# Softmax sums folded over partitions by accumulating DMAs, and kept in two running sums

## The chip, the cores and the metric

One core of one Trainium2 chip. The metric is the device time of one launch in microseconds (us). The run times and the profile of the kernel before are given below. Engines are named as in the profile: PE is TensorE (PEld its weight loads), DVE is VectorE, ACT is ScalarE, POOL is GpSimd, SP is SyncE, which only issues DMAs here.

## The reference, cut to what matters

Two graph layers over 16 images of 1024 nodes and 256 channels. The change concerns the attention of the first layer (4 heads of 64 channels), its softmax above all:

```python
h = jnp.maximum(_layernorm(x, axis=-1), 0.0)
# layer 0: q from a graph product with adj, k and v from h @ kv_w
q = jnp.transpose(g, (0, 2, 1)).reshape(B, N, h, hd).transpose(0, 2, 1, 3)
scale = (1.0 + 1e-06) / (np.sqrt(hd) + 1e-06)
attn = jax.nn.softmax(jnp.einsum('bhnd,bhmd->bhnm', q, k) * scale, axis=-1)
out = jnp.einsum('bhnm,bhmd->bhnd', attn, v)
# then x = x + out; layer 1: another layernorm, A_hat @ h, two linear layers with batch norms
```

The kernel takes the exps without subtracting a maximum, multiplies them with v, and divides by their sum at the end. Smallest and largest inverse sum are kept (`most`, `least`), and a general version runs afterwards if they leave a safe range.

## The kernel before, in words

The kernel is one long loop over the images b. The order of instructions on every engine is written out by hand: what the program says first on an engine runs first there, and an instruction that waits holds all that stand behind it on that engine. Data lies transposed: in the scores, the partitions are the keys m (8 blocks of 128), and the free axis holds 2 heads x 512 queries.

Attention of one image has four steps, each for half of the queries (g = 0, 1) and a pair of heads. Step s does this:

- `scores(s)` (L743 to L760): for each of the eight key blocks, TensorE computes the scores into PSUM (`f_s`), ScalarE takes the exp into `f_p` (128x1024, eight buffers), and VectorE adds the blocks up into `f_acc` (128x1024, two buffers): one add of two blocks (L757), and six that each add to the same running sum (L760).
- `partial(s)` (L768, L776): `f_acc` holds, per partition, the sum over 8 keys; the sum over the 128 partitions remains. VectorE transposes blocks of 32x32 (128x1024 to `f_sums`) and reduces over 32. That leaves four partial sums for each query, one per group of 32 partitions (`f_red`).
- `values(s)` (L784, L797): TensorE multiplies the exps with v into `f_o`, and VectorE transposes the product into `f_oT`.

`finish(g)` inverts the sums of one half and scales: `collect` (four ScalarE copies bring the four groups' sums side by side on 32 partitions, L811), `invert` (VectorE: reduce L817, reciprocal L818, `most` and `least`), `spread` (four ScalarE copies bring the inverses to the partitions that need them, L826), `scale` (VectorE multiplies `f_oT`, L835, and SyncE moves blocks of 32 partitions to their places with 16 DMAs, L852) and `add` (VectorE, L860). For g = 0 they run in the middle of step 2 and at its end; those of g = 1, with the `add` of g = 0, are handed on as `left` to what follows attention.

What follows is the graph product of the next image, `graph` for b = 0 and `graph_seven` for b = 1 to 14. `graph_seven` is a Strassen-like scheme of seven products: ScalarE and VectorE make eight weight blocks (`differences(b, c)`, then `masked(b, c)`, L361), VectorE forms the sums t1 to t4 of them (L557 to L569), and TensorE runs `plain(0)`, `plain(1)` (L514) and then the products `m1` to `m_7` (L576), in an order given in the source. In VectorE's order stand `masked(b, 2)`, `masked(b, 3)`, then `collect` and `invert` of the attention just done, then `masked(b, 4)`, the t sums, `masked(b, 5)` and on to `scale` and `masked(b, 7)`. At its start, SyncE is given loads: `sums_h` (buffer tag "sums"), `sums_c` (in a buffer of tag "acc"), two blocks of hT, para, `sums`, and with `load_more` six blocks of 512 KB (L915). After it come the keys and values, the linear layers of the image before (`linear1`, `linear1_seven`), and the next attention. For the last image (b = 15) no graph product is left, and `collect` and `invert` stand before `sums_of_h` of `linear1`.

GpSimd does little: the inverse roots of the norms (L260), and stores and copies of DMAs (`turn_h`, L379; `pair_sums`, L482; `turn_h_aside`, L496).

Of the kernel before, what the change touches and what calls it, by code (L numbers as in the profile page):

```python
# [10 lines left out]
F32 = mybir.dt.float32  # L11
AF = mybir.ActivationFunctionType
ALU = mybir.AluOpType
AX = mybir.AxisListType
# [15 lines left out]
def fast_path(  # L30
# [62 lines left out]

    RECS = HEADS * 512 // 32
    most = const.tile([32, RECS], F32, tag="most", name="f_most")
    nc.vector.memset(most, 1.0)
    least = const.tile([32, RECS], F32, tag="least", name="f_least")
    nc.vector.memset(least, 1.0)
# [77 lines left out]
    with ExitStack() as stage:  # L176
# [324 lines left out]
        def graph_seven(b, left, norm, load_more, last):  # L501
# [26 lines left out]
            nc.sync.dma_start(sums_h, gs_d[b][:, 0:8].rearrange("p (s n) q -> p s n q", s=4))  # L528
            nc.sync.dma_start(sums_c, gs_d[b][:, 8:12])
            hT = []  # L530
# [4 lines left out]
            qT = big.tile([P, CC, N], F32, tag="qT", name=f"f_qT_{b}")  # L535
            nc.sync.dma_start(qT, para_v)
            nc.sync.dma_start(sums, kvs_d)
            load_more()
            kT = big.tile([P, CC, N], F32, tag="kT", name=f"f_kT_{b}")
# [192 lines left out]
        def attention(b, qT, kT, v, hooks):  # L732

            steps = [(g, pair) for g in range(NH) for pair in range(HEADS // 2)]
            p_of, acc_of, oT_of, o_of, red_of = {}, {}, {}, {}, {}

            def scores(s, within=None):
                g, pair = steps[s]
                for m in range(NC):
# [13 lines left out]
                    if m == 1:  # L753
                        acc = pp.tile(
                            [P, 2, 512], F32, tag="acc", name=f"f_acc_{b}_{s}", bufs=2
                        )
                        nc.vector.tensor_add(acc, p_of[s, 0], p)  # L757
                        acc_of[s] = acc
                    elif m > 1:
                        nc.vector.tensor_add(acc_of[s], acc_of[s], p)  # L760
                    if m == 5 and within:
                        within()

            def partial(s):

                g, pair = steps[s]
                t = ow.tile([P, 2, 16, 32], F32, tag="sums", name=f"f_sums_{b}_{s}")
                nc.vector.transpose(  # L768
                    t.rearrange("p e j i -> p (e j i)"),
                    acc_of.pop(s).rearrange("p e q -> p (e q)"),  # L770
                )
                if pair == 0:
                    red_of[g] = small.tile(
                        [P, HEADS // 2, 2, 16], F32, tag="red", name=f"f_red_{b}_{g}", bufs=1
                    )
                nc.vector.tensor_reduce(red_of[g][:, pair], t, AX.X, ALU.add)  # L776

# [24 lines left out]
            def finish(g):  # L802
# [4 lines left out]
                def collect():  # L807
                    t = ow.tile([32, RECS, 4], F32, tag="parts", name=f"f_parts_{b}_{g}")
                    red = red_of.pop(g).rearrange("p h e j -> p (h e j)")
                    for a in range(4):  # L810
                        nc.scalar.copy(t[:, :, a], red[ts(a, 32), :])  # L811
                    kept["parts"] = t

                def invert():
                    t = small.tile([32, HEADS // 2, 2, 16], F32, tag="rec", name=f"f_rec_{b}_{g}")
                    every = t.rearrange("p h e j -> p (h e j)")
                    nc.vector.tensor_reduce(every, kept["parts"], AX.X, ALU.add)  # L817
                    nc.vector.reciprocal(every, every)  # L818
                    nc.vector.tensor_tensor(most, most, every, ALU.max)
                    nc.vector.tensor_tensor(least, least, every, ALU.min)  # L820
                    kept["rec"] = t

                def spread():
                    t = small.tile([P, HEADS // 2, 4, 4], F32, tag="recs", name=f"f_recs_{b}_{g}")
                    for a in range(4):
                        nc.scalar.copy(  # L826
                            t[ts(a, 32)].rearrange("p h j c -> p h c j"),
                            kept["rec"][:, :, a // 2].rearrange("p h (c j) -> p h c j", c=4),
                        )
                    kept["recs"] = t  # L830
# [37 lines left out]
            for i in range(len(steps)):  # L868
                scores(i, collect if i == 2 else None)
                for step in hooks.get(i, ()):  # L870
                    step()
                if i == 2:
                    invert()
                    spread()
                partial(i)
                if i == 2:
                    scale()
                values(i)
# [419 lines left out]
        with tc.manual_schedule(engines={ENG.PE, ENG.Activation, ENG.DVE, ENG.Pool, ENG.SP}):  # L1298
# [73 lines left out]
            for b in range(B):  # L1372
# [15 lines left out]
                def more(c):  # L1388
# [4 lines left out]
                    0: [  # L1393
                        lambda: turn_h(b + 1), more(2), left[0], left[1], left[2], more(3),
                        left[3], left[4], more(4),
                    ],
# [94 lines left out]
    with ExitStack() as stage:  # L1491
# [21 lines left out]
        with tc.manual_schedule(engines={ENG.PE, ENG.Activation, ENG.DVE, ENG.Pool, ENG.SP}):  # L1513
# [118 lines left out]
            def flag_bad():  # L1632

                bad = const.tile([32, 4], F32, tag="bad", name="f_bad")
                nc.vector.tensor_reduce(bad[:, 0:1], most, AX.X, ALU.max)
# [735 lines left out]
```

## Time and profile before

| | |
|---|---|
| median of 3 runs | 2397.92 us (2396.44 to 2398.54) |
| span of the profiled execution | 2396.9 us |
| what lies around that span, if it is taken as a median run | 1.0 us |
| one image in the middle (856.21 to 987.40 us) | 131.2 us: TensorE busy 131.0, VectorE 112.2, ScalarE 73.2, GpSimd 9.4 |
| of it attention, four steps | 56.3 us |
| mean clock granted to TensorE | 0.995 |
| transposes and reduces of the sums (L768, L776) | 64 each, 79.2 and 78.1 us of VectorE |

The page gives busy time per engine, 40 slices of the span, the chain of work that ended last, the costliest groups of instructions (line, engine, operation, output from inputs, shapes, count, then busy time and mean ns of one, then the engine's idle time before them and what ended it) and the DMA issues (output from input, issuing queue, count, KB each, median us from issue to landing). A timeline has start and length in us, then engine, line, operation, tiles and count; in square brackets stands the idle time before, and what ended it. "SPq" and "POOLq" are DMAs issued by SyncE and GpSimd.

### The profile page before, as it was taken

What the parts mean: (1) busy time and instruction counts of PE and PEld (TensorE: products, weight loads), DVE (VectorE), ACT (ScalarE), POOL (GpSimd) and SP (SyncE); (2) the same over time, 40 slices, a digit from 0 to 9 for tenths busy, and PEclk for the clock granted to TensorE, in tenths of its full rate; (3) what the DMA queues carried; (4) which work ended last, traced back from release to release, by engine and by line L of the source; (5) the groups of instructions that cost most, each with busy time, mean ns of one, the idle gap of its engine ahead of it and who ended that gap; (6) DMA issues with size and microseconds to landing.
All of it is one profiled execution on the core that took longest, in us unless ns stands there. A gap on an engine that the chain in (4) does not pass through costs nothing.

```text
span 2396.9 us, 24478 instructions
## 1 busy us (share of the span) xinstructions
PE 2353.8 (98%) x7950; PEld 1032.4 (43%) x7950; DVE 1974.2 (82%) x2806; ACT 1346.8 (56%) x1974; POOL 174.1 (7%) x253
## 2 busy tenths in 40 slices
PE   8999999999999999999999999999999999999995
PEld 4443444434343434444343434344443434444444
DVE  6888889797979798897979797988979798757766
ACT  6845555564736455555647374555555565346654
POOL 2030010101010000101010100001010100000000
PEclk9999999999999999999999999999999999999998
DMA  5042433433342434334323414243433321355569
GB/s 189 8 143 93 144 116 123 136 117 91 98 156 64 160 93 160 100 123 136 120 96 111 140 61 164 87 167 93 137 123 121 115 85 53 114 208 181 174 243 371
DMA packets 178650, 312.44 MB, mean 130 GB/s; under 512 B 33617, under 2 KB 117073, under 8 KB 178513
## 3 DMA queue, kind: packets, MB, share of 16 engines
q1 hardware_dynamic: 164176, 267.25, 33.2%
q0 software_dynamic: 9728, 26.76, 3.7%
q10 hardware_dynamic: 4608, 16.78, 1.7%
q8 instruction: 65, 1.06, 0.2%
q14 instruction: 73, 0.59, 0.1%
HBM read 195.04 MB, written 96.79 MB: 122 GB/s over the span
## 4 chain that ended last, share of the span: by engine, by line
PE 72%; DVE 18%; ACT 4%; issue 3%; DMA 1%; SPq 1%; DVEq 0%; ACTq 0%; POOLq 0%; POOL 0%
PE f_aps L944 16%; PE f_s L743 12%; PE f_o L784 11%; PE f_zps L1050 6%; DVE f_acc L760 6%; PE f_vps L450 5%; PE f_zx L1588 4%; DVE f_w L361 4%; PE f_gpsx L576 3%; PE f_zm L1588 3%; ACT f_p L751 3%; PE f_gps L576 3%; PE f_kpsx L691 2%; PE f_gps L404 2%; PE f_kps L691 2%
## 5 line engine op out<-in xcount | busy, mean ns | idle before, releaser
L751 ACT ACTIVATE f_p<-f_s 128x1024 f32<-128x1024 f32 x512 | 477.4, 1048 | 163.0 <-PE f_s L743 163.0
L760 DVE TENSOR_TENSOR f_acc<-f_acc,f_p 128x1024 f32<-128x1024 f32 x384 | 470.5, 1225 | 41.4 <-DVE f_acc L760 1.4
L743 PE MATMUL f_s<-f_qT,f_kT 64*128 64x512 f32 x2048 | 457.1, 596 | 0.0
L784 PE MATMUL f_o<-f_p,f_v 128*64 128x512 f32 x2048 | 453.6, 595 | 0.0
L743 PEld LDWEIGHTS f_s<-f_qT,f_kT 64*128 64x128 f32 x2048 | 190.2, 185 | 264.4 <-ACT f_p L751 118.6
L784 PEld LDWEIGHTS f_o<-f_p,f_v 128*64 128x64 f32 x2048 | 141.4, 137 | 304.4 <-issue 251.3
L353 ACT ACTIVATE f_w<-f_row,f_col 128x1024 f32<-128x1024 f32 x127 | 147.0, 1157 | 31.6 <-PE f_gps L514 16.8
L361 DVE SCALAR_TENSOR_TENSOR f_w<-f_w,f_adj 128x1024 f32<-128x1024 f32 x127 | 152.7, 1212 | 4.2 <-ACT f_w L356 4.2
L260 POOL TENSOR_TENSOR f_rstd_b<-f_var_b,f_mhalf 128x4 f32<-128x4 f32 (+1 forms) x31 | 33.1, 1069 | 1502.3 <-DVE f_var_b L259 1502.3
L356 ACT ACTIVATE f_w<-f_w 128x1024 f32<-128x1024 f32 x127 | 134.3, 1058 | 4.0
L944 PE MATMUL f_aps<-f_ahatT,f_hs 128*128 128x512 f32 x256 | 115.1, 592 | 0.0
L944 PE MATMUL f_aps<-f_ahatT,f_h_b 128*128 128x512 f32 x256 | 113.4, 596 | 0.0
L450 PE MATMUL f_vps<-f_kvw,f_hT 128*128 128x256 f32 x512 | 113.1, 379 | 0.0
L944 PE MATMUL f_aps<-f_t,f_hs 128*128 128x512 f32 x256 | 112.5, 592 | 0.0
L281 ACT ACTIVATE f_h_b<-f_x,f_shift_b,f_rstd_b 128x256 f32<-128x256 f32 x128 | 66.3, 593 | 75.7 <-DVE f_shift_b L266 75.7
L450 PEld LDWEIGHTS f_vps<-f_kvw,f_hT 128*128 128x128 f32 x512 | 97.3, 190 | 20.1 <-issue 7.4
L281 ACT ACTIVATE f_h_a<-f_x,f_shift_a,f_rstd_a 128x256 f32<-128x256 f32 x126 | 73.8, 587 | 50.5 <-DVE f_shift_a L266 50.5
L514 PE MATMUL f_gps<-f_w,f_h_a 128*128 128x512 f32 x224 | 99.9, 599 | 0.0
L757 DVE TENSOR_TENSOR f_acc<-f_p,f_p 128x1024 f32<-128x1024 f32 x64 | 76.3, 1192 | 14.4 <-ACT f_p L751 14.4
L576 PE MATMUL f_gps<-f_w,f_h_a 128*128 128x512 f32 x168 | 82.7, 601 | 3.8 <-DVE f_w L361 3.8
L1073 ACT ACTIVATE f_z<-f_zps,f_b 128x512 f32<-128x512 f32 x60 | 38.0, 683 | 75.3 <-PE f_zps L1050 75.3
L776 DVE TENSOR_REDUCE f_red<-f_sums 128x32 f32<-128x1024 f32 x64 | 78.1, 1220 | 2.2
(275 smaller groups left out, 3410.6 us busy)
## 6 DMA issues: line engine op xcount, KB each, us to landing
f_t<-ft SPq DMA_DIRECT2D x84, 512.0 KB, 10.9
fz<-f_z SPq DMA_DIRECT2D x64, 512.0 KB, 9.6
f_x<-in_x_dram SPq DMA_DIRECT2D x31, 1024.0 KB, 6.3
f_zb<-fz SPq DMA_DIRECT2D x42, 512.0 KB, 4.2
f_att<-f_oT SPq DMA_DIRECT2D x512, 32.0 KB, 1.9
fx<-f_x SPq DMA_DIRECT2D x16, 1024.0 KB, 4.4
fhT<-f_hQ POOLq DMA_DIRECT2D x112, 128.0 KB, 2.9
f_hT<-fhT SPq DMA_DIRECT2D x28, 512.0 KB, 6.0
```

The costliest lines, as they stand in the source:

```text
L281: nc.scalar.activation(self.h[:, c, :], self.xt[:, c, :], AF.Relu, bias=self.shift[:, c : c + 1], scale=self.rstd[:, c : c + 1], accum_out ...
L353: nc.scalar.activation(w, rows[b], AF.Abs, bias=cols[b][:, c : c + 1], scale=0.5 / C)
L361: nc.vector.scalar_tensor_tensor(w, w, 1.0, adj_t[c], ALU.subtract, ALU.mult)
L450: nc.tensor.matmul(ps[:, i, :], hT[e][:, ts(c4 + i, P)], kvw_t[:, e, C : 2 * C], start=(e == 0), stop=(e == CC - 1),)
L576: nc.tensor.matmul(ps, left, right, start=fresh and n == 0, stop=(n == PAIRS - 1), skip_group_check=more,)
L743: nc.tensor.matmul(ps[:, e, :], kT[rows_e, pair, ts(m, P)], qT[rows_e, pair, ts(g, 512)], start=True, stop=True,)
L751: nc.scalar.activation(p, ps, AF.Exp)
L760: nc.vector.tensor_add(acc_of[s], acc_of[s], p)
L784: nc.tensor.matmul(o_of[s][e * HD : (e + 1) * HD, :], v[:, m, ts(2 * pair + e, HD)], p[:, e, :], start=(m == 0), stop=(m == NC - 1),)
L944: nc.tensor.matmul(ps, left[:, m, :], right(m), start=not more and m == 0, stop=(m == KH - 1), skip_group_check=more,)
L1050: nc.tensor.matmul(ps[i], left[:, ts(i, P)], right, start=not more, stop=True, skip_group_check=more,)
L1588: nc.tensor.matmul(ps, left[:, m, :], right[:, m, :], start=start and m == 0, stop=(m == 1), skip_group_check=not start,)
```

## The change

- `scores` keeps two running sums: even blocks in `f_acc`, odd ones from block 3 on in `flat` (a tile of tag "sums"); one more add joins them at the end, so there are seven adds as before. Steps that the caller hangs in (`hooks`) now come before that last add, and `within` is called at the last block of every step.
- A new `fold(s)`, after `scores(s)`: `f_acc` (128x1024) is seen as four groups of 32 partitions and four quarters of 256 elements. Four DMAs of SyncE copy group a's quarter a into a tile of 128x256 (`f_fold`); then twelve accumulating DMAs of GpSimd, in three rounds of four, add the other groups' same quarter to it. Each moves 32 partitions x 256 elements (32 KB).
- `partial(s)` works on 128x256 and runs one step later, at the last block of step s + 1, where its input is the folded tile. For the last step it is called by `collect`.
- `collect` no longer copies anything; `invert` only takes the reciprocal, on 128 partitions x 16 elements; `spread` makes eight copies of 16 elements rather than four of 32. `most`, `least` and `bad` lie on 128 partitions.
- In `graph_seven`, `sums_c` is loaded after the hT and para loads and after `load_more`, since its buffer is the one that the last `f_acc` leaves. For b = 0 the order around `collect` is changed: three weights come before it, and `turn_h` goes after `spread`.

```diff
--- before.py
+++ after.py
@@ -91,10 +91,11 @@
     LASTING = ["z"] * 4 + [None] * 2 + ["w2n", "w2T"]
 
 
-    RECS = HEADS * 512 // 32
-    most = const.tile([32, RECS], F32, tag="most", name="f_most")
+    QUARTER = 2 * 512 // 4
+    RECS = HEADS // 2 * QUARTER // 32
+    most = const.tile([P, RECS], F32, tag="most", name="f_most")
     nc.vector.memset(most, 1.0)
-    least = const.tile([32, RECS], F32, tag="least", name="f_least")
+    least = const.tile([P, RECS], F32, tag="least", name="f_least")
     nc.vector.memset(least, 1.0)
 
     class BatchNorm:
@@ -526,7 +527,6 @@
             sums_h = ow.tile([P, 4, 2, P], F32, tag="sums", name=f"f_gs_{b}")
             sums_c = rest[:, 0].rearrange("p (s q) -> p s q", s=4)
             nc.sync.dma_start(sums_h, gs_d[b][:, 0:8].rearrange("p (s n) q -> p s n q", s=4))
-            nc.sync.dma_start(sums_c, gs_d[b][:, 8:12])
             hT = []
             for d in range(CC):
                 t = pp.tile([P, N], F32, tag="p", name=f"f_hT_{b}_{d}")
@@ -534,8 +534,9 @@
                 hT.append(t)
             qT = big.tile([P, CC, N], F32, tag="qT", name=f"f_qT_{b}")
             nc.sync.dma_start(qT, para_v)
+            load_more()
+            nc.sync.dma_start(sums_c, gs_d[b][:, 8:12])
             nc.sync.dma_start(sums, kvs_d)
-            load_more()
             kT = big.tile([P, CC, N], F32, tag="kT", name=f"f_kT_{b}")
             v = big.tile([P, NC, C], F32, tag="v", name=f"f_v_{b}")
             room = v.rearrange("p (n k) c -> p n (k c)", n=4)
@@ -732,9 +733,9 @@
         def attention(b, qT, kT, v, hooks):
 
             steps = [(g, pair) for g in range(NH) for pair in range(HEADS // 2)]
-            p_of, acc_of, oT_of, o_of, red_of = {}, {}, {}, {}, {}
-
-            def scores(s, within=None):
+            p_of, acc_of, fold_of, oT_of, o_of, red_of = {}, {}, {}, {}, {}, {}
+
+            def scores(s, within=None, before_last=()):
                 g, pair = steps[s]
                 for m in range(NC):
                     ps = ps_s.tile([P, 2, 512], F32, tag="s", name=f"f_s_{b}_{s}_{m}")
@@ -756,24 +757,46 @@
                         )
                         nc.vector.tensor_add(acc, p_of[s, 0], p)
                         acc_of[s] = acc
-                    elif m > 1:
-                        nc.vector.tensor_add(acc_of[s], acc_of[s], p)
-                    if m == 5 and within:
+                    elif m == 3:
+                        odd = ow.tile([P, 2, 16, 32], F32, tag="sums", name=f"f_sums_{b}_{s}")
+                        flat = odd.rearrange("p e j i -> p e (j i)")
+                        nc.vector.tensor_add(flat, p_of[s, 2], p)
+                    elif m > 3:
+                        to = flat if m % 2 else acc_of[s]
+                        nc.vector.tensor_add(to, to, p)
+                    if m == NC - 1:
                         within()
+                for step in before_last:
+                    step()
+                nc.vector.tensor_add(acc_of[s], acc_of[s], flat)
+
+            def fold(s):
+
+                acc = acc_of[s].rearrange("p e q -> p (e q)")
+                t = ow.tile([P, QUARTER], F32, tag="parts", name=f"f_fold_{b}_{s}")
+                fold_of[s] = t
+
+                def part(a, r):
+                    return acc[ts((a + r) % 4, 32), ts(a, QUARTER)]
+
+                for a in range(4):
+                    nc.sync.dma_start(t[ts(a, 32), :], part(a, 0))
+                for r in range(1, 4):
+                    for a in range(4):
+                        nc.gpsimd.dma_start(t[ts(a, 32), :], part(a, r), accum_op=ALU.add)
 
             def partial(s):
 
                 g, pair = steps[s]
-                t = ow.tile([P, 2, 16, 32], F32, tag="sums", name=f"f_sums_{b}_{s}")
-                nc.vector.transpose(
-                    t.rearrange("p e j i -> p (e j i)"),
-                    acc_of.pop(s).rearrange("p e q -> p (e q)"),
-                )
+                t = acc_of.pop(s).rearrange("p e q -> p (e q)")[:, 0:QUARTER]
+                nc.vector.transpose(t, fold_of.pop(s))
                 if pair == 0:
                     red_of[g] = small.tile(
-                        [P, HEADS // 2, 2, 16], F32, tag="red", name=f"f_red_{b}_{g}", bufs=1
-                    )
-                nc.vector.tensor_reduce(red_of[g][:, pair], t, AX.X, ALU.add)
+                        [P, HEADS // 2, QUARTER // 32], F32, tag="red", name=f"f_red_{b}_{g}", bufs=1
+                    )
+                nc.vector.tensor_reduce(
+                    red_of[g][:, pair], t.rearrange("p (j i) -> p j i", i=32), AX.X, ALU.add
+                )
 
             def values(s):
                 g, pair = steps[s]
@@ -805,17 +828,14 @@
                 kept = {}
 
                 def collect():
-                    t = ow.tile([32, RECS, 4], F32, tag="parts", name=f"f_parts_{b}_{g}")
-                    red = red_of.pop(g).rearrange("p h e j -> p (h e j)")
-                    for a in range(4):
-                        nc.scalar.copy(t[:, :, a], red[ts(a, 32), :])
-                    kept["parts"] = t
+                    partial(NH * g + 1)
 
                 def invert():
-                    t = small.tile([32, HEADS // 2, 2, 16], F32, tag="rec", name=f"f_rec_{b}_{g}")
-                    every = t.rearrange("p h e j -> p (h e j)")
-                    nc.vector.tensor_reduce(every, kept["parts"], AX.X, ALU.add)
-                    nc.vector.reciprocal(every, every)
+                    t = small.tile(
+                        [P, HEADS // 2, QUARTER // 32], F32, tag="rec", name=f"f_rec_{b}_{g}"
+                    )
+                    every = t.rearrange("p h j -> p (h j)")
+                    nc.vector.reciprocal(every, red_of.pop(g).rearrange("p h j -> p (h j)"))
                     nc.vector.tensor_tensor(most, most, every, ALU.max)
                     nc.vector.tensor_tensor(least, least, every, ALU.min)
                     kept["rec"] = t
@@ -823,10 +843,15 @@
                 def spread():
                     t = small.tile([P, HEADS // 2, 4, 4], F32, tag="recs", name=f"f_recs_{b}_{g}")
                     for a in range(4):
-                        nc.scalar.copy(
-                            t[ts(a, 32)].rearrange("p h j c -> p h c j"),
-                            kept["rec"][:, :, a // 2].rearrange("p h (c j) -> p h c j", c=4),
-                        )
+                        for half in range(2):
+                            nc.scalar.copy(
+                                t[ts(a, 32), :, :, 2 * half : 2 * half + 2].rearrange(
+                                    "p h j c -> p h c j"
+                                ),
+                                kept["rec"][ts(a // 2 * 2 + half, 32)].rearrange(
+                                    "p h (c j) -> p h c j", c=2
+                                ),
+                            )
                     kept["recs"] = t
 
                 def scale():
@@ -866,13 +891,18 @@
             first = finish(0)
             collect, invert, spread, scale, add = first
             for i in range(len(steps)):
-                scores(i, collect if i == 2 else None)
-                for step in hooks.get(i, ()):
-                    step()
+
+                def within():
+                    if i == 2:
+                        collect()
+                        invert()
+                    elif i > 0:
+                        partial(i - 1)
+
+                scores(i, within, hooks.get(i, ()))
+                fold(i)
                 if i == 2:
-                    invert()
                     spread()
-                partial(i)
                 if i == 2:
                     scale()
                 values(i)
@@ -1391,8 +1421,8 @@
                 norm = Norm(xr[b], f"b{b}")
                 between = {
                     0: [
-                        lambda: turn_h(b + 1), more(2), left[0], left[1], left[2], more(3),
-                        left[3], left[4], more(4),
+                        more(2), left[0], more(3), more(4), left[1], left[2], left[3],
+                        lambda: turn_h(b + 1), left[4],
                     ],
                     1: [more(5)],
                     2: [more(6), lambda: norm.stats(0, 4)],
@@ -1631,7 +1661,7 @@
 
             def flag_bad():
 
-                bad = const.tile([32, 4], F32, tag="bad", name="f_bad")
+                bad = const.tile([P, 4], F32, tag="bad", name="f_bad")
                 nc.vector.tensor_reduce(bad[:, 0:1], most, AX.X, ALU.max)
                 nc.vector.tensor_reduce(bad[:, 1:2], least, AX.X, ALU.min)
                 nc.vector.tensor_scalar(bad[:, 2:3], bad[:, 0:1], LIMIT, None, ALU.is_gt)
```

## The prediction

> **What bounds the kernel now.** First the page's busy table, then the stretch of one image in order of time, engine by engine (image 6, attention from 856 us; the fourteen images from 1 to 14 repeat it every 131.2 us).
>
> ```profile
> PE 2353.8 (98%) x7950; PEld 1032.4 (43%) x7950; DVE 1974.2 (82%) x2806; ACT 1346.8 (56%) x1974; POOL 174.1 (7%) x253
> ```
>
> TensorE is busy all the time; VectorE, which the change relieves, is not the bound. TensorE's timeline shows how little it waits.
>
> ```profile
> 898.39 7.14 PE L743 MATMUL f_s<-f_qT,f_kT 64*128 64x512 f32 x32
> 905.46 7.09 PE L784 MATMUL f_o<-f_p,f_v 128*64 128x512 f32 x32
> 912.48 7.13 PE L514 MATMUL f_gps<-f_w,f_h_a 128*128 128x512 f32 x16
> ...
> 927.17 1.02 PE L576 MATMUL f_gpsx<-f_w,f_h_a 128*128 128x512 f32 x2
> 928.38 1.13 PE L576 MATMUL f_gps<-f_w,f_h_a 128*128 128x512 f32 x2 [0.18 <-DVE f_w L361]
> ```
>
> Attention steps follow each other every 14.08 us without a hole, and so does the rest. Pairs of matmuls start every 0.86 us, so the last pair was due at 928.03 and started at 928.38: 0.35 us lost to VectorE, waiting for the last masked weight (`m2(2)`, after `masked(b, 7)`). Laid out by matmul starts, this place loses 7.5 us over the fourteen images (0.33 to 0.72 each, and 0.1 of restart). That is all that a lighter VectorE can give back.
>
> VectorE in the same stretch has no hole from 861 to 932 us:
>
> ```profile
> 903.52 7.87 DVE L760 TENSOR_TENSOR f_acc<-f_acc,f_p 128x1024 f32<-128x1024 f32 x6
> 911.43 1.25 DVE L768 STREAM_TRANSPOSE f_sums<-f_acc 128x1024 f32<-128x1024 f32 x1
> 912.71 1.22 DVE L776 TENSOR_REDUCE f_red<-f_sums 128x32 f32<-128x1024 f32 x1
> 913.84 0.71 DVE L797 STREAM_TRANSPOSE f_oT<-f_o 128x512 f32<-128x512 f32 x1
> 914.47 2.32 DVE L361 SCALAR_TENSOR_TENSOR f_w<-f_w,f_adj 128x1024 f32<-128x1024 f32 x2
> 916.71 0.40 DVE L817 TENSOR_REDUCE f_rec<-f_parts 32x64 f32<-32x256 f32 x1
> ...
> 927.11 1.22 DVE L361 SCALAR_TENSOR_TENSOR f_w<-f_w,f_adj 128x1024 f32<-128x1024 f32 x1
> ```
>
> The reader should see the distance from the last sum (911.4) to the inversion of the group's sums (`invert`, 916.71): 5.3 us, and that 11.6 us of unbroken work follow, at whose end TensorE already stands waiting. Whatever delays `invert` beyond 916.35 delays TensorE one for one.
>
> SyncE's queue, and the two DMA groups of the fold's very shape (32 partitions of 1 KB, SBUF to SBUF):
>
> ```profile
> 901.71 11.26 SPq L852 DMA_DIRECT2D f_att<-f_oT  x16
> 913.95 0.33 SPq L528 DMA_DIRECT2D f_gs<-fgs  x1
> ...
> 916.95 5.06 SPq L915 DMA_DIRECT2D f_t<-ft  x6
> ```
> ```profile
> f_att<-f_oT SPq DMA_DIRECT2D x512, 32.0 KB, 1.9
> f_hT<-f_hQ POOLq DMA_DIRECT2D x32, 32.0 KB, 1.7
> ```
> ```profile
> L379 POOL DMA_DIRECT2D f_hT<-f_hQ x32 | 15.7, 500 | 3.0 <-PE f_gps L404 3.0
> ```
>
> A 32 KB copy lands 1.9 us after its issue on SyncE and 1.7 us on GpSimd; GpSimd spends 0.5 us issuing each, SyncE 0.64.
>
> [...]the SyncE copies' landings range from 1.8 to 7.8 us[...].
>
> **The change, part by part.**
>
> *VectorE per step.* Out: a transpose and a reduce of 128x1024, 1.24 + 1.22. In: both at 128x256, taken at 0.43 each. Adds stay seven; alternating between two sums they follow each other every 1.14 to 1.2 us where the chained ones needed 1.31 (7.87/6). VectorE is lighter by 1.6 to 2.4 us of each step, 100 to 150 us in all, but TensorE's 14.08 us per step does not depend on it: worth at most the 7.5 us above.
>
> *ScalarE.* `collect` loses its four copies of 0.31 us, `spread` grows from four to eight of about 0.24: no one waits for ScalarE there, nothing.
>
> *When the last fold can start.* The exps of step 3 end at 907.1 (eight in 7.44 us from 899.63), one per 0.92. The pairing add of p2 and p3 can start at 903.4; five adds of 1.2 end at 909.4, `partial(2)` takes 0.85, the joining add 1.22: 911.4, as today, because the exps and not VectorE's backlog now set it. SyncE: fold 2's four copies go out ahead of the sixteen f_att copies, whose 11.3 us of issue then run from about 900.4 to 911.7. Fold 3's four follow: the last is issued at 913.6 and lands at 915.5.
>
> *The chain.* Then three accumulates for each group, each round waiting for the landing of the one before. Their price is not in the trace: from below 1.7 us (the plain copy; less is excluded, since an accumulate also moves these bytes), from above 4.5 (a landing held up by the 5 MB that SyncE starts to load at 914). I take 2.5, which is 2.4 to land and 0.1 to wake the queue; the four groups run side by side, since GpSimd needs 4 x 0.5 = 2.0 us to issue a round. Landed at 915.5 + 3 x 2.5 = **923.0**.
>
> *The new wait.* `collect()` now is `partial(3)`, in VectorE's queue behind `masked(b, 3)`. VectorE, rid of 2.5 us, gets there at about 915.5 and stands until 923.0. Behind it stand `invert`, `masked(b, 4)` and every t sum; for those wait TensorE's `m_7(0)`, `m1(1)` and all after; ScalarE's `spread` waits as well. From landing to `masked(b, 4)` it is 0.43 + 0.43 + 0.25 + 0.35 = 1.4 us against 1.3 from L817 today. So VectorE runs 923.0 - 916.7 + 0.1 = 6.4 us late, and TensorE with it: 14 x 6.4 = 90 us.
>
> *Ends.* Image 15: `sums_of_h` stands behind the same wait, TensorE takes its s2 at 2064.8 today; by the same offset it is ready at about 2071: 6 us. Image 0 has three more weights ready before `collect`, and `turn_h`, moved behind it with 32 GpSimd copies (16 us of issue), is read at 149.5: about 3 us together.
>
> *Moved loads.* sums_c now waits for `partial(3)` (924) behind six 512 KB loads that land up to 933; its first readers are due at 931.1 + 6.4 = 937.5: covered. If the fold were quick (920) that cover is gone and some 1 us would show. The hT and para loads shift by 0.3 us, read at 938 and later, nothing. GpSimd's rstd (due at 937) stands behind the twelve accumulates, covered. Folds 0 to 2 have 12 us until the next step's `partial`: 2.6 of issue, 1.9, 3 x 1.9 make 10.2, covered by under 2 us.
>
> Sum: 90 + 6 + 3 = 99 us on the profile's span of 2396.9 (the runs' median is 1.0 more): 2397.9 + 99 = **2497 us**.
>
> **Rivals.** (1) *Crowded fold*: rounds of 4.1 us, because the loads share the engines or an accumulate costs GpSimd 1 us to issue. Landed at 928; 14 x 11.3 + 17 = 175: 2573; and `partial` would stall in the middle steps too. For: landings up to 7.8 us. Against: the accumulates have a queue of their own. (2) *Quick fold*: 1.75 us a round, landed at 920.7: 14 x 4.1 + 5 = 62: 2460. For: thirty-two copies in a row kept 1.7. Against: those had no loads beside them. (3) *Hidden fold, faster*: landed before 916.3, TensorE never waits for `m2(2)`: -7.5, 2390. It decides from a fold of 4.9 us; four landings one after the other make 7 at the least. (4) *The wait is there and TensorE has slack for it*, no change: the 0.35 us of waiting at 928.38 speaks against it.
>
> **Chances.** Forecast 0.52 (2460 to 2540), crowded 0.24, quick 0.17, hidden 0.05, no change 0.02. Range 2440 to 2590: half of the crowded case lies above its middle, and a quick fold begun 1 us earlier gives 2444. About 0.2% is what a measurement of this kernel tells from no change. Faster 0.05, same 0.02, slower 0.93.
>
> **What would show it.** After: VectorE idle 5 to 12 us before the small transpose in the graph stage, released by a DMA; TensorE's hole in L576 of 5 to 8 us per image; attention still 14.08 us per step; the accumulates 2 to 3 us from issue to landing. Wrong if the last accumulate lands within 5 us of the joining add, or if attention steps themselves grow (then the middle folds are late, too).

## The result, and the profile after

The changed kernel takes **2821.07 us**, median of 5 runs (2817.68 to 2826.81), against 2398.37 for the kernel before beside it: a ratio of 1.1767 (95% interval 1.1753 to 1.178). It is 423 us slower where the forecast said 99. The profiled execution spans 2816.7 us, at a mean clock granted to TensorE of 0.933 (0.995 before).

The page's busy table and the engine shares of its chain:

```profile
PE 2431.4 (86%) x7950; PEld 1057.6 (38%) x7950; DVE 1830.2 (65%) x2774; ACT 1343.0 (48%) x1974; POOL 780.6 (28%) x1021
...
PE 42%; DMA 22%; DVE 14%; POOL 12%; issue 6%; ACT 2%; SPq 0%; DVEq 0%; POOLq 0%; ACTq 0%
```

VectorE is 144 us lighter, within the 100 to 150 expected. But a third of the chain that ended last is now DMA and GpSimd, and nearly all of that is the fold (20% and 12% by line).

To see where the time went, each image is cut at the starts of its matmul groups (medians over the images, us):

| | steps 0, 1, 2 | step 3 | graph product | keys and values | linear layers | image | first image | last image to the end |
|---|---|---|---|---|---|---|---|---|
| before | 14.09 each | 14.09 | 25.46 | 13.21 | 36.2 | 131.2 | 134.7 | 395.7 |
| after | 14.09 each | **21.55** | **45.6** | 13.20 | 36.2 | 158.9 | 147.4 | 420.6 |

Fourteen images lose 20.1 us each in the graph product (282) and 7.5 in step 3 (104); the ends lose 12.7 and 24.9. That makes 424, against 420 between the two spans. The forecast had 6.4 in the graph product, nothing in step 3, and 9 at the ends. At the end of the last image 16.6 us are one wait of TensorE for `sums_of_h`, which stands behind the last fold; the forecast had 6 there. Attention steps that grow were one of the forecast's own signs of being wrong, with the middle folds late; step 3 shows it.

**The graph product.** VectorE's timeline in one image, then TensorE's (start, length, engine, line, operation; idle time before it and what ended it):

```profile
875.82 0.45 DVE L792 STREAM_TRANSPOSE f_acc<-f_fold 128x256 f32<-128x256 f32 x1 [3.20 <-DMA f_fold<-f_acc]
...
892.50 0.45 DVE L792 STREAM_TRANSPOSE f_acc<-f_fold 128x256 f32<-128x256 f32 x1 [5.79 <-DMA f_fold<-f_acc]
...
909.66 1.22 DVE L771 TENSOR_TENSOR f_acc<-f_acc,f_sums 128x1024 f32<-128x1024 f32 x1
...
911.43 2.32 DVE L362 SCALAR_TENSOR_TENSOR f_w<-f_w,f_adj 128x1024 f32<-128x1024 f32 x2
934.41 0.45 DVE L792 STREAM_TRANSPOSE f_acc<-f_fold 128x256 f32<-128x256 f32 x1 [20.67 <-DMA f_fold<-f_acc]
...
944.94 1.22 DVE L362 SCALAR_TENSOR_TENSOR f_w<-f_w,f_adj 128x1024 f32<-128x1024 f32 x1
```
```profile
896.62 6.26 PE L744 MATMUL f_s<-f_qT,f_kT 64*128 64x512 f32 x20 [3.73 <-ACT f_p L752]
...
918.51 1.02 PE L577 MATMUL f_gps<-f_w,f_gs 128*128 128x512 f32 x2
937.78 2.05 PE L577 MATMUL f_gps<-f_kT,f_gs 128*128 128x512 f32 x2 [18.24 <-DVE f_kT L558]
...
946.21 1.12 PE L577 MATMUL f_gps<-f_w,f_h_a 128*128 128x512 f32 x2 [0.26 <-DVE f_w L362]
```

The new wait is where the forecast put it: at `collect`, which is `partial(3)`, released by the last fold's DMA, with the t sums behind it and TensorE behind those. Only it lasts 20.67 us, not 7.5. The joining add (L771) ends at 910.88; the last accumulate lands just before 934.4, so the fold takes 23.5 us from there, where 11.6 was forecast.

The fold itself shows on GpSimd's timeline, first for step 1 of this image, then for step 3:

```profile
881.32 9.57 POOL L786 DMA_DIRECT2D f_fold<-f_acc  x12 [7.17 <-DMA f_fold<-f_acc]
```
```profile
913.27 3.14 POOL L786 DMA_DIRECT2D f_fold<-f_acc  x4 [6.21 <-DMA f_fold<-f_acc]
917.89 0.77 POOL L786 DMA_DIRECT2D f_fold<-f_acc  x1 [1.47 <-DMA f_fold<-f_acc]
919.66 0.77 POOL L786 DMA_DIRECT2D f_fold<-f_acc  x1 [1.01 <-DMA f_fold<-f_acc]
924.03 3.14 POOL L786 DMA_DIRECT2D f_fold<-f_acc  x4 [3.61 <-issue]
930.42 1.56 POOL L786 DMA_DIRECT2D f_fold<-f_acc  x2 [3.25 <-DMA f_fold<-f_acc]
```

Step 1: GpSimd issues twelve accumulates without a hole, in 9.57 us, 0.80 each; its issue alone sets the length. Step 3: between the groups it waits for landings, which take 4.3 to 6.7 us for all but the last two. In that time SyncE starts the graph product's loads:

```profile
910.91 2.47 SPq L783 DMA_DIRECT2D f_fold<-f_acc  x4
913.42 0.58 SPq L529 DMA_DIRECT2D f_gs<-fgs  x1
914.11 0.84 SPq L533 DMA_DIRECT2D f_hT<-fhT  x2
...
915.53 3.88 SPq L945 DMA_DIRECT2D f_t<-ft  x6
```

Thirteen images have all these loads. In them 98 of the 104 accumulates of the second and third round start 0.28 to 0.29 us after the one before in their group has landed: the last fold is a chain of landings, as the forecast had assumed.

**Step 3.** Nobody was to wait for ScalarE. Its timeline says otherwise:

```profile
893.72 1.80 ACT L847 COPY f_recs<-f_rec 32x16 f32<-32x16 f32 x8 [9.15 <-DVE f_rec L838]
895.54 3.77 ACT L752 ACTIVATE f_p<-f_s 128x1024 f32<-128x1024 f32 x4
```

`spread` stands in ScalarE's queue ahead of the exps of step 3. It waits for the inverses, these for `partial(1)`, and that for the fold of step 1, which is late (the 5.79 us at 892.50). TensorE has scores waiting for their exps from 892.9 on, and stops (3.73 us).

Fold 1 is late in two ways. It is long (13.2 us), and it begins late: VectorE already waits for fold 0 (the 3.20 us at 875.82), and step 1's joining add, with which fold 1 begins, stands behind that wait. On the median of fourteen images fold 0 has 10.6 us from its first copy until VectorE is ready for it, and VectorE waits 4.0 us; fold 1 then has only 7.4 us, and VectorE waits 6.1.

**The clock.** The windows of one image by TensorE's clock (PEclk):

```profile
core 0: us, PE busy (x) PEld busy (x) DVE busy (x) ACT busy (x) POOL busy (x), PEclk, DMA share, GB/s
...
897.00:901.00 4.00, 4.00 (x13) 1.67 (x11) 2.90 (x4) 3.34 (x4) 3.56 (x6) 0.57 0.42 75
909.00:913.00 4.00, 4.00 (x14) 1.51 (x11) 3.97 (x6) 1.62 (x2) 0.00 (x0) 1.00 0.08 21
937.00:941.00 4.00, 3.22 (x4) 1.51 (x5) 3.93 (x7) 3.90 (x6) 0.00 (x0) 0.50 0.01 2
```

After either stop, TensorE runs at about half speed for some 4 us. So a stop costs more than its own length: the step 3 shown here loses 5.7 us to a stop of 3.73. Over the fourteen images step 3 loses 7.5 us on the mean to stops of 5.2, and the graph product 20.3 (against its 25.08 us without any stop, e1 below) to stops of 17.6. With the two stops shown, of 3.73 and 18.24 us, the clock is at 0.50 for 3.4 and 3.9 us of the work that follows (0.57 is the mean of the whole window from 897 to 901).

### The profile page after: what moved, and what is told of

Read it like the earlier page. It is cut to its first block, busy times and chain, and to the rows that moved or that the text cites. A ratio compares the mean times of both kernels' runs of the same rounds, so it can differ in the third digit from the quotient of the medians.

```text
span 2816.7 us, 26050 instructions
## 1 busy us (share of the span) xinstructions
PE 2431.4 (86%) x7950; PEld 1057.6 (38%) x7950; DVE 1830.2 (65%) x2774; ACT 1343.0 (48%) x1974; POOL 780.6 (28%) x1021
## 3 DMA queue, kind: packets, MB, share of 16 engines
q0 software_dynamic: 46592, 51.97, 10.6%
## 4 chain that ended last, share of the span: by engine, by line
PE 42%; DMA 22%; DVE 14%; POOL 12%; issue 6%; ACT 2%; SPq 0%; DVEq 0%; POOLq 0%; ACTq 0%
DMA f_fold<-f_acc 20%; PE f_aps L974 13%; POOL f_fold L786 12%; PE f_gps L577 4%; PE f_vps L451 4%; PE f_zx L1618 3%; PE f_gpsx L577 3%; PE f_zps L1080 3%; PE f_zm L1618 3%; DVE f_w L362 2%; DVE f_acc L771 2%; PE f_kpsx L692 2%; DVE f_st L1119 2%; PE f_kps L692 1%; DVE f_z L1110 1%
## 5 line engine op out<-in xcount | busy, mean ns | idle before, releaser
L786 POOL DMA_DIRECT2D f_fold<-f_acc x768 | 605.0, 1249 | 824.1 <-DMA f_fold<-f_acc 653.1
L744 PE MATMUL f_s<-f_qT,f_kT 64*128 64x512 f32 x2048 | 493.4, 632 | 79.8 <-ACT f_p L752 79.8
L792 DVE STREAM_TRANSPOSE f_acc<-f_fold 128x256 f32<-128x256 f32 x64 | 28.5, 445 | 520.5 <-DMA f_fold<-f_acc 520.5
L744 PEld LDWEIGHTS f_s<-f_qT,f_kT 64*128 64x128 f32 x2048 | 202.1, 198 | 368.7 <-ACT f_p L752 191.4
L847 ACT COPY f_recs<-f_rec 32x16 f32<-32x16 f32 x256 | 55.3, 216 | 447.6 <-DVE f_rec L838 444.9
L577 PE MATMUL f_gps<-f_kT,f_gs 128*128 128x512 f32 x56 | 42.9, 859 | 242.7 <-DVE f_kT L558 242.7
L766 DVE TENSOR_TENSOR f_acc<-f_acc,f_p 128x1024 f32<-128x1024 f32 x128 | 155.8, 1217 | 5.8 <-ACT f_p L752 5.8
L766 DVE TENSOR_TENSOR f_sums<-f_sums,f_p 128x1024 f32<-128x1024 f32 x128 | 155.8, 1217 | 3.2 <-ACT f_p L752 2.9
L974 PE MATMUL f_aps<-f_t,f_hs 128*128 128x512 f32 x256 | 114.9, 602 | 16.6 <-DVE f_hs L959 16.6
L577 PEld LDWEIGHTS f_gps<-f_kT,f_gs 128*128 128x128 f32 x56 | 12.4, 251 | 261.0 <-issue 259.3
L451 PEld LDWEIGHTS f_vps<-f_kvw,f_hT 128*128 128x128 f32 x512 | 97.3, 190 | 20.1 <-issue 6.7
## 6 DMA issues: line engine op xcount, KB each, us to landing
f_t<-ft SPq DMA_DIRECT2D x84, 512.0 KB, 11.6
```

Of the source, the lines that this page charges most:

```text
L451: nc.tensor.matmul(ps[:, i, :], hT[e][:, ts(c4 + i, P)], kvw_t[:, e, C : 2 * C], start=(e == 0), stop=(e == CC - 1),)
L577: nc.tensor.matmul(ps, left, right, start=fresh and n == 0, stop=(n == PAIRS - 1), skip_group_check=more,)
L744: nc.tensor.matmul(ps[:, e, :], kT[rows_e, pair, ts(m, P)], qT[rows_e, pair, ts(g, 512)], start=True, stop=True,)
L766: nc.vector.tensor_add(to, to, p)
L786: nc.gpsimd.dma_start(t[ts(a, 32), :], part(a, r), accum_op=ALU.add)
L974: nc.tensor.matmul(ps, left[:, m, :], right(m), start=not more and m == 0, stop=(m == KH - 1), skip_group_check=more,)
```

## Experiments

My theory after the result: the mechanism of the forecast holds, and the fold is too long, because an accumulate costs GpSimd more than a copy and because the loads slow its landing; step 3 is a second wait, behind fold 1. The rivals: the DMA traffic itself slows the engines; the two running sums cost something; one of the two prices explains it all. All ratios are against the kernel before, with 95% intervals.

Two measures are used below: the length of a fold, from its first SyncE copy to its last landing (median over the sixteen images), and the stages of the table above.

### e1: the two running sums alone

```diff
-                    elif m > 1:
-                        nc.vector.tensor_add(acc_of[s], acc_of[s], p)
+                    elif m == 3:
...
+                        nc.vector.tensor_add(flat, p_of[s, 2], p)
+                    elif m > 3:
+                        to = flat if m % 2 else acc_of[s]
+                        nc.vector.tensor_add(to, to, p)
+                nc.vector.tensor_add(acc_of[s], acc_of[s], flat)
```

> The kernel before with the two running sums alone (no fold; sums transposed and reduced at 128x1024 at once). Theory: alternating adds follow each other every 1.14 us instead of 1.31, so the last sum of an image is done about 1 us earlier and TensorE's 0.35 to 0.72 us of waiting for the last weight of the graph product goes: 5 to 7.5 us less, 2391 to 2393 us. Rival: the joining add comes after the last exp and puts the sum 1.2 us later: up to 14 x 1.2 = 17 us more, 2398 to 2415 us.

Measured: 2391.26 us, ratio 0.9972 (0.9961 to 0.9982), graph product 25.08 us. The sums give back 6.5 us of the 7.5 that the forecast allowed to a lighter VectorE. All of the loss lies with the fold and what was moved for it. This is the fastest kernel of the study.

### e2: the fold for steps 0 and 1 only

The two running sums stay. Steps 2 and 3 keep the transpose and reduce of before, and the loads their old order; so no fold lies in the graph product.

```diff
                 scores(i, within, hooks.get(i, ()))
-                fold(i)
+                if i < 2:
+                    fold(i)
...
+                if i > 1:
+                    partial(i)
```

> Two running sums; the fold only for steps 0 and 1 (the half g = 0); steps 2 and 3 transposed and reduced at 128x1024 at once, loads in the order of before. Theory: the loss in the graph product (20.1 us an image) belongs to the last fold and goes; step 3 keeps its 7.5 us, because ScalarE's spread stands behind the fold of step 1, which takes 13.2 us: 2398 + 14 x 7.5 + about 10 at both ends = 2513 us. Rival: step 3 is slow because of the fold of step 2 and of the copies of f_att beside it; then about 2398 us.

Measured: 2504.42 us, ratio 1.0448 (1.0432 to 1.0464). The graph product is back at 25.08 us, step 3 stays at 20.89. ScalarE's and TensorE's timelines in one image:

```profile
939.09 1.81 ACT L886 COPY f_recs<-f_rec 32x16 f32<-32x16 f32 x8 [11.18 <-DVE f_rec L877]
```
```profile
942.00 3.79 PE L744 MATMUL f_s<-f_qT,f_kT 64*128 64x512 f32 x8 [5.78 <-ACT f_p L752]
```

So step 3's loss belongs to folds 0 and 1 and needs neither fold 2 nor fold 3 nor the loads: fold 0 delays fold 1 here, too (on the median VectorE waits 3.4 us and then 6.1). The rival, fold 2 with the copies of f_att beside it, falls.

### e3: the DMAs without anyone who waits

The kernel before, and in each step three copies by SyncE (the fold has four) and twelve accumulates by GpSimd, of the fold's size, into partitions of a tile that nobody reads.

```diff
+            def shadow(s):
...
+                for a in range(1, 4):
+                    nc.sync.dma_start(both[ts(a, 32), :], part(a, 0))
+                for r in range(1, 5):
+                    for a in range(1, 4):
+                        nc.gpsimd.dma_start(both[ts(a, 32), :], part(a, r), accum_op=ALU.add)
...
                 partial(i)
+                shadow(i)
```

> The kernel before, and in each step beside it three copies by SyncE and twelve accumulating DMAs by GpSimd (four rounds of three) from an idle tile into a scratch tile that no one reads. Theory: only the wait for the fold costs, not its DMAs: 2398 us, at most 10 more where the copies hold up SyncE's loads; the accumulates themselves take 1.35 us to issue and 2.8 us to land as in the changed kernel, 5 us or more beside the graph product's loads. Rival: the DMAs [...] slow VectorE or the memory: tens of us more, VectorE's operations longer.

Measured: 2402.23 us, ratio 1.0018 (1.0011 to 1.0024). In the fourteen middle images every stage is as before; the 4.5 us lie at the two ends. VectorE's adds to the running sum take 1.225 us each in both kernels. The rival that the traffic slows the engines falls: what costs is waiting for it.

### e4: sums_c ahead of the other loads again

```diff
             nc.sync.dma_start(sums_h, gs_d[b][:, 0:8].rearrange("p (s n) q -> p s n q", s=4))
+            nc.sync.dma_start(sums_c, gs_d[b][:, 8:12])
...
-            nc.sync.dma_start(sums_c, gs_d[b][:, 8:12])
```

> The changed kernel with the load of sums_c back in its old place, ahead of hT, para and the six 512 KB blocks: SyncE then waits there for the last partial, so that those loads (5 MB) do not run beside the last fold. Theory: the last fold falls from 22.6 to about 13.5 us, VectorE goes on some 9 us earlier, the graph product loses about 11 us an image in place of 20: 2821 - 14 x 9 = 2690 us. Rival: the accumulates are slow by themselves or by their number, and the loads' place does not matter: 2821 us, or more because the loads come late.

Measured: 2814.84 us, ratio 1.1746 (1.1728 to 1.1764), fold 3 still 22.7 us. The expectation missed, because the edit did not do what it was for: I took sums_c to wait for `partial(3)`, but it lies in the buffer that step 2's sum leaves, so SyncE did not stop there (in one image it issued sums_c at 913.7, and `partial(3)` came at 934.1) and the large loads started as early as ever. It also means that the forecast's sentence on sums_c, and the reason given with the change for moving that load, were wrong, at no price.

### e5: the loads behind the last inverses

A small DMA of the inverses to DRAM makes SyncE wait for them; all loads but sums_h go behind it.

```diff
+            def loads():
+                nc.sync.dma_start(sums_c, gs_d[b][:, 8:12])
...
+                load_more()
...
+                    if g == 1:
+                        nc.sync.dma_start(gate_d, every)
```

> The changed kernel with the loads of sums_c, hT, para, kvs and the six 512 KB blocks put behind the inversion of the last half's sums: a small DMA of the inverses stands ahead of them on SyncE and waits for it. (In the run before, sums_c turned out to lie in the buffer of step 2's sum, so SyncE did not wait.) Theory: without those 5 MB beside it the last fold takes 13.3 us as the others do, not 22.6; VectorE goes on about 9.5 us earlier: 2821 - 14 x 9.5 = 2688 us. Rival: the last fold is slow without them, too, or the loads, now late, are waited for: 2790 us or more.

Measured: 2707.27 us, ratio 1.1285 (1.1266 to 1.1304). Fold 3 takes 14.9 us instead of 22.6, its accumulates land in 3.1 us on the mean instead of 5.6, and the graph product takes 37.7 us instead of 45.6. Loads beside the fold cost 114 us. Step 3 (21.2) is untouched. The time is 19 us above the expectation, which had the fold at 13.3 us.

### e6 and e8: plain copies in place of accumulates

Number, size, order and waits of the DMAs are those of the accumulates; what is left out is the adding, so that of the four groups' sums only the last copied stays. e6 is the changed kernel with this edit, e8 is e5 with it.

```diff
-                        nc.gpsimd.dma_start(t[ts(a, 32), :], part(a, r), accum_op=ALU.add)
+                        nc.gpsimd.dma_start(t[ts(a, 32), :], part(a, r))
```

> The changed kernel with plain copies in place of the accumulates: the same sixteen DMAs, waits and order, but the other three groups' sums are overwritten and not added. Theory: a plain copy costs GpSimd 0.5 us and lands in 1.7, so a fold of steps 0 to 2 takes about 9 us, VectorE no longer waits in the steps and step 3 is back at 14.1 us (14 x 7 = 98 us less); beside the loads the last fold still takes some 16 us and the graph product loses about 13 us an image: about 2600 us. Rival: the crowding is of the accumulates alone; then the last fold lands in some 12 us and the time is my forecast, about 2500 us.

> Both: plain copies (the other groups' sums are overwritten and not added) and the loads behind the inversion. Theory: this is the chain that I forecast, 1.9 + three rounds of about 2.2: the last fold some 9 us, VectorE on at about 920, the graph product 3 to 5 us late: 2398 + 14 x 4 + 10 = about 2464 us. Rival: the wait has another cause than price and crowd; then above 2550 us.

Measured: e6 2657.08 us, ratio 1.1081 (1.1062 to 1.11); e8 2529.92 us, ratio 1.0545 (1.0527 to 1.0562). The four kernels, with their times in us, fold 1, fold 3, step 3 and graph product:

| | loads beside fold 3 | loads behind it |
|---|---|---|
| accumulates | after: 2821 (13.2, 22.6, 21.55, 45.6) | e5: 2707 (13.2, 14.9, 21.2, 37.7) |
| plain copies | e6: 2657 (10.4, 21.0, 14.09, 43.0) | e8: 2530 (10.3, 11.8, 14.09, 33.9) |

The two prices add up within 13 us: the loads cost 114 or 127 us, the accumulates 164 or 177. Neither explains it alone. They lie in different places: in the graph product the loads cost 7.9 or 9.1 us an image and the accumulates 3.8 or 2.6, in step 3 the loads cost 0.4 or nothing and the accumulates 7.5 or 7.1. e6 came out 57 us above its expectation, since beside the loads the fold of plain copies takes 21.0 us and not 16. The page's groups for the DMAs of GpSimd, of after and of e8 (busy us, mean ns of one):

```profile
L786 POOL DMA_DIRECT2D f_fold<-f_acc x768 | 605.0, 1249 | 824.1 <-DMA f_fold<-f_acc 653.1
```
```profile
L791 POOL DMA_DIRECT2D f_fold<-f_acc x768 | 378.6, 498 | 799.4 <-DMA f_fold<-f_acc 584.5
```

The engine's time for one is 0.79 us against 0.49 (605.0 and 378.6 over 768; the mean of after is longer because its records overlap: 1.35 us each by the median, started 0.80 us apart). With plain copies VectorE waits 0.8 us for fold 0, fold 1 begins in time and takes 10.3 us where it has 10.1 (medians of e8), and VectorE's wait for it is 0.9 us. TensorE has slack for that, and step 3 is whole again: in step 3 it is the accumulate's price that counts.

e8 is the forecast's own case: its fold 3 takes 11.8 us, where 11.6 was assumed. The wait that costs TensorE most there, and then the same wait in after (us in total, times, longest):

```profile
PE f_gps L581 <- DVE f_kT L562: 86.2, 14, 8.9
```
```profile
PE f_gps L577 <- DVE f_kT L558: 242.7, 14, 18.8
```

86.2 over 14 is 6.2 us per image, against 6.4 forecast. Yet the graph product lost 8.8 us against e1. The other 2.6 are nearly all clock: in one image, of the matmuls that follow the stop one starts 0.56 us late and four 0.42 us late each, 2.3 us together, and the clock stands at 0.50 for 4 us. Over the fourteen images 2.6 us each make 37 of the 66 us by which e8 missed its expectation; the rest is the fold, 11.8 us where I had expected 9.

### e7: e2 with spread behind the exps of step 3

```diff
+                    elif i == 3:
+                        spread()
+                        scale()
...
-                if i == 2:
-                    spread()
...
-                if i == 2:
-                    scale()
```

> As e2 (fold for steps 0 and 1 alone), with spread and scale of the first half moved from the end of step 2 to the end of step 3's scores. Theory: step 3 lost its 7 us because ScalarE's spread, ahead of step 3's exps in its queue, waited for the fold; moved behind them it costs TensorE nothing: step 3 back at 14.1 us, 2504 - 105 = about 2398 us. Rival: VectorE's own waits for the folds of steps 0 and 1 hold up step 3: about 2500 us.

Measured: 2569.21 us, ratio 1.0715 (1.0697 to 1.0732): 65 us slower than e2, where all of e2's loss was to go. Step 3 did fall, from 20.9 to 15.9 us (median; 17.5 on the mean), so `spread`, which moved with `scale`, was most of what held it. But the graph product rose from 25.1 to 33.0. TensorE's two largest waits:

```profile
PE f_gps L577 <- DMA f_gs<-fgs: 65.8, 12, 6.4
PE f_o L821 <- DVE f_oT L834: 35.4, 16, 4.3
```

The first is in the graph product: `scale` sends sixteen copies (f_att), 10 us of SyncE's issue, and at their new place they go out ahead of sums_h, which TensorE needs. The second is what is left in step 3: VectorE still waits for fold 1 at `partial(1)`, ahead of the joining sum and the transpose of f_o, and holds TensorE that way.

### e9: e7 with those copies behind the loads

The multiplication stays where e7 has it, the sixteen copies move.

```diff
             nc.sync.dma_start(sums, kvs_d)
+            move0()
             load_more()
```

> The kernel of e7 (two running sums; fold for steps 0 and 1 only; the spread of the inverses behind the exps of step 3), with one more edit: the sixteen copies that move the scaled halves of f_oT to f_att go out behind the graph product's small loads (sums_h, sums_c, hT, para, kvs) instead of ahead of them. In e7 the trace has these copies on SyncE from 977.9 to 988.1 us of one image, the load of sums_h at 988.26, and TensorE waiting 4.29 us for that load. Theory: of e7's graph stage of 33.0 us, the 8 us over the 25.1 of the two sums alone come from that order; so the graph stage falls back to 25 to 26.5 us, step 3 stays at 15.9, and the time is 2569 - 14 x 7.5 - about 5 for the ends = 2459, within 2440 to 2475. Rival: the graph stage is long because VectorE comes late out of step 3 (its joining sum stands behind the wait for fold 1), and the load only happens to arrive then: the graph stage stays over 31 us, and the time over 2540.

Measured: 2571.76 us, ratio 1.073 (1.0715 to 1.0744): no gain over e7. The stage did what the theory said: the graph product fell to 27.2 us, and the wait for f_gs is gone. Step 3 did not gain (17.3 us on the mean). But the keys and values rose from 13.2 to 17.3 us and the linear layers from 36.2 to 37.9. TensorE's waits of e9, then VectorE's:

```profile
PE f_aps L1031 <- ACT f_v L459: 52.2, 13, 6.0
PE f_o L822 <- DVE f_oT L835: 35.3, 16, 4.3
```
```profile
DVE f_x L940 <- DMA f_att<-f_oT: 116.4, 29, 8.1
```

The copies of both halves now stand one after the other on SyncE, 30 us of issue; VectorE's adds of f_att wait for them, and behind VectorE ScalarE's f_v and TensorE's linear product. The expectation of 2459 missed since I looked for the next wait in the stage that I repaired and not in the one that the copies were moved into.

## Why the prediction was wrong

- **The bound and the gain: right.** TensorE bounds the kernel, and a lighter VectorE is worth 6.5 us (e1), within the 7.5 worked out.
- **Place and mechanism of the new wait: right.** `collect` waits for the last fold and TensorE for VectorE, and with a fold of about the assumed length (11.8 us) the wait is 6.2 us against 6.4 (e8). Only "one for one" was not so: for these 6.2 us the graph product lost 8.8.
- **The small prices on VectorE: right.** Transpose 0.45, reduce 0.42, reciprocal 0.25 us, where the forecast's estimates were 0.43, 0.43 and 0.25 (a TENSOR_TENSOR of 128x256 took 426 ns in the trace of before, L481); the joining add ended at 910.9, forecast 911.4.
- **The step that failed is "I take 2.5" for a round of accumulates.** From the joining add to the last landing it is 23.5 us in place of 11.6. Two terms were mis-sized. "GpSimd needs 4 x 0.5 = 2.0 us to issue a round": it needs 3.14, 0.79 for each, against landings of 2.8 on the mean (fold 1), so that the issue and not the landing sets a fold without those loads beside it, and it takes 13.2 us. And "2.4 to land" is 5.6 with the loads beside it, above even the upper bound of 4.5. Both were my estimates, though the slowest f_att copy of before took 7.8. With the 0.28 to start the next, a round of the last fold is 5.9 us and not 2.5. The crowded rival had both reasons, but at rounds of 4.1, and a chance of 0.24. What I held against it, that accumulates have a queue of their own, counted for nothing: in that queue they landed in 5.6 us on the mean beside the loads, against 3.1 without them (e5). The 16 DMA engines were busy for 0.93 of the time around fold 3 (after, 913 to 934), and for 0.31 around fold 1 (880 to 893).
- **"Folds 0 to 2 ... covered by under 2 us": wrong.** They take 13.2 to 14.4 us, and the 12 us were not there: fold 0 had 10.6, and as VectorE's wait for it delays fold 1, that had 7.4. And **"no one waits for ScalarE there, nothing": wrong.** I had named what stands behind the wait on VectorE, but not what stands behind `spread`: the exps of step 3. Together they are step 3's 104 us, as e2, e6 and e7 show.
- **A restart after the new stop: left out.** The forecast saw 0.1 us of restart after stops of under 1 us and added nothing for a stop of 6. In the changed kernel the slow stretch after a stop costs 2.7 us in the graph product and 2.3 in step 3 (the losses less the stops, above): 14 x 5.0 = 70 us.
- **The sum, per image, in the graph product:** the forecast's wait 6.2, the restart 2.6 (both e8), the accumulates' price 3.8 (e5 less e8), the loads 7.9 (after less e5), less the 0.4 that the two sums give back (e1): 20.1, and 20.1 measured. These are differences from one kernel to the next, so that they must add up; by way of e6 in place of e5 the accumulates are 2.6 and the loads 9.1.

**What stays open.** GpSimd stands idle from 920.4 to 924.0 in the fold shown, 2.9 us longer than the landing explains, and the profile names no releaser. Two of the thirteen images have such a hole, and their folds are hardly longer than the others (23.3 us, where the others take 22.2 to 23.5). Why an accumulate takes longer to issue isn't settled: the page's queue table gives 48 packets to each against 32 to a plain copy (36864 and 24576 more packets than in the kernel before, over 768), which goes with 0.79 against 0.49 us but proves nothing. Whether the loads hold up the landings in the DMA engines or at the memory isn't settled. A fold in fewer rounds wasn't tried.

## What to carry to other kernels

Price a chain of DMAs by the issue time of its queue as well as by its landings, and take the landing from a place where the same large loads run beside it. For every wait that an edit adds, go through the queue of each engine that waits, ScalarE's and SyncE's copies too, and ask what stands behind; e7 and e9 show that moving a late step only chooses who pays. Where TensorE is the bound and stops for several microseconds, add the slow stretch after the stop (2 to 3 us here).

## What the runs showed of the hardware

- An accumulating DMA of 32 KB within SBUF took GpSimd 0.79 us of issue; away from the graph product's loads (fold 1, after) it landed in 2.0 to 3.8 us, 2.8 on the mean. A plain copy took 0.49 us and landed in 1.65 to 4.0, 1.9 on the mean (fold 1, e6 and e8).
- Beside 5 MB of loads, landings rose from 3.1 to 5.6 us on the mean with accumulates (e5 and after), and from 2.2 to 4.9 with plain copies (e8 and e6): a queue of their own protected neither.
- After each of TensorE's 28 stops of 3.7 to 18.8 us in the middle images of after, its clock was 0.50 for 3.1 to 5.9 us of the work that followed. In the first image it was 0.50 for 3.2 and 6.1 us after stops of 2.66 and 3.23 us, and stayed at 1.00 after one of 1.47 us.
